# A four-layer graph network on one core: four of sixteen terms of the per-node sum moved to ScalarE and Pool, and the later layers' weights made inside an earlier product

## The chip, the cores and the metric

One core of a Trainium2 chip runs the whole program. The metric is the device time of one execution in microseconds (us). Five engines work side by side: TensorE (PE) multiplies matrices, VectorE (DVE) and ScalarE (ACT) work element by element, GpSimd (POOL) does some of that too and here issues most stores, SyncE (SP) issues loads. Each takes its instructions in a fixed order; a semaphore holds an instruction until its inputs are there and its output buffer is free. Matmul results lie in PSUM, everything else on chip in SBUF.

## The reference

Eight graphs of N = 2048 nodes with C = 64 features share one matrix A, the rows of `adj`. Each layer takes h = relu(layernorm(x)) and adds its result to x. Layer 0, which the change is about:

```python
w = jnp.einsum('nd,dkio->nkio', embedding, weight)      # D = 16, K = 3
b = jnp.einsum('nd,do->no', embedding, bias)
As = [I, A, 2.0 * (A @ A) - I]
x_g = jnp.einsum('knm,bmc->bnkc', jnp.stack(As), x)     # x is h here
out = jnp.einsum('bnki,nkio->bno', x_g, w) + b
```

So each node n has a weight of its own, a sum over d of `embedding[n, d]` times a common weight. Layer 1 runs three steps v = W2 relu(W1 [v, A v] + b1) + b2, layer 2 is A h with a linear map behind it, layer 3 is attention. All three come down here to products with A, small weight matrices and, in layer 3, a mean over the nodes. The weights that layers 1 and 2 use (products of W1, W2 and w_out, and their bias rows) don't depend on x; the program makes them once, in `make_weights`.

## The kernel before

**Tiling.** Two graphs side by side make a pair, since 2×64 features fill 128 partitions; there are NP = 4 pairs p. The nodes come in NB = 4 blocks nb of 512, a block being four tiles t of 128 nodes. A stays in SBUF as `BT`. `product` (L212) makes one block of A v for a pair: 32 matmuls, 16 chunks by two, since v is split into a high and a low part, `H` and `L` (`halves`, L199: ScalarE casts, VectorE subtracts). Its result in PSUM is scaled by the row `crow` (L209) on VectorE.

**Layer 0 of a pair.** First `term1` (L344): four products, which give t1 = A h for all nodes; each block is transposed back and split again for the second product. In pairs 2 and 3 this is a stage by itself; for pairs 0 and 1 the prologue makes t1. Then for each block nb: the product that gives t2 = A t1, then `node_weights` (L565). There, for each tile t and each half dg of the 16 values of d, PE makes

```python
y = psums[-1].tile([P, 2, 512], F32, tag="big", ...)    # two such buffers, L576
y[:, bb, :] = sum over k of terms[k][hs_, ts] x wt[hs_, k, dg * 512:(dg + 1) * 512]
```

that is, for 128 nodes and both graphs, what eight values of d would give (8×64 columns). Twelve matmul instructions make one y. Then VectorE adds the eight parts up, each scaled by the node's own embedding value, a column of one value per partition (L589):

```python
xj = (av, ov)[d % 2][:, t]                              # acc for even d, odd for odd d
nc.vector.scalar_tensor_tensor(xj, yd, ec, old, op0=ALU.mult, op1=ALU.add)
```

`acc` starts as x (loaded by `load_x`), `odd` starts as the bias block `bn` (loaded from `biasD`, two buffers). After the four tiles L597 adds `odd` to `acc`, and `keep` (L556) begins the norm for the next layer and stores x to `xs`. So a block has eight y tiles, and a layer 0 of 16 blocks 128 of them and 1,024 sums. The last block of all is different: between its tiles `prepare_next` already prepares layer 1.

**The norm.** `norm_stages` (L152) is a generator of three stages: mean and z (VectorE) and the square (ScalarE); the variance (VectorE) and `rstd` (a power on Pool, L169); z times rstd with the relu (L172), then the store of z to `hs` from Pool's queue. A stage is emitted whenever `go_on` (L182) is called: after a product and after each tile of `node_weights`.

**What sets the order.** The Tile framework places the instructions on each engine in the order in which the program emits them. `tc.issue_after(ins)` moves what is emitted inside it behind a named instruction, which then decides its place: `go_on` puts the norm's stages behind the last sum, and the store of the mask `MD` (L648) stands behind the store of `xs`. Waits follow from tiles: a reader waits for the writer, and the writer of a reused buffer for the readers of its last contents. Loads are on SP, in order (x, bias block, crow rows, h blocks); stores of `hs`, `xs`, `MD` and `wD` are issued by Pool, in order, between its own arithmetic.

**The weights.** `make_weights` (L471) is called once, for pair 3 ahead of block 1's product, and put behind the last sum of block 0 (`chain[-1]`):

```python
if p == NP - 1 and nb == 1:
    with tc.issue_after(chain[-1].ins):
        make_weights()
```

It loads eight columns and eight weight blocks (into `raw`, cleared by Pool first, L479), transposes them on PE (pt_wT, L484), copies them on VectorE (`tr`), multiplies four pairs on PE (wP, L490), copies the result (`pr`, L491), adds `b1s` (L493), loads the row `b_out` (L496) over what raw held and adds it (L497), and stores three parts to `wD` from Pool's queue (L504 to L506). Layers 1 and 2 load `wD` later. `raw`, `tr` and `pr` take the three buffers of the tag "z", which the norm's z uses as well; the PSUM tag "tr" has two buffers for all transposes.

Of the kernel before, what the change touches and what calls it, by code (L numbers as in the profile page):

```python
# [8 lines left out]
F32 = mybir.dt.float32  # L9
# [4 lines left out]
AF = mybir.ActivationFunctionType  # L14
ALU = mybir.AluOpType
# [27 lines left out]
def uniform_path(  # L43
# [30 lines left out]
    nc = tc.nc  # L74
    P = 128
    B, N, C = x.shape
    NP = B // 2
# [3 lines left out]
    DG = 512 // C  # L81
# [13 lines left out]
    hs = [dram.tile([P, NCH, 2 * C], F32, name=f"hs{p}") for p in range(NP)]  # L95
# [8 lines left out]
    def block(tag, name, bufs):  # L104

        return work.tile([P, 4, 2 * C], F32, tag=tag, name=name, bufs=bufs)
# [8 lines left out]
    def part(nb):  # L115
        return slice(4 * nb, 4 * nb + 4)
# [61 lines left out]
    def norm_relu(xt, name, done, out_=None):  # L178
        n = norm_stages(xt, name, done, out_)
        next(n)  # L180
        pending.append([n, 2])
# [12 lines left out]
        while pending:  # L194
            go_on()

    copies = []

    def halves(src, name, pool=None):  # L199

# [24 lines left out]
    def transposed(src, name):  # L225

        pt = psums[-1].tile([P, 4, P], F32, tag="tr", name=f"pt_{name}")
        for t in range(4):
            nc.tensor.transpose(pt[:, t, :], src(t), ident)  # L229
        return pt  # L230
# [11 lines left out]

    def term(k, name):
        pool = l0t if k == 1 else l0f[0]
        return pool.tile([P, 512], F32, tag=f"t{k}", name=name, bufs=(2, 4, 2)[k])

    def norm_0(p, nb, also=None, xt=None):

        def done(z):
            nc.gpsimd.dma_start(hs[p][:, part(nb), :], z)  # L250
            if also is not None:
                also(z)

        norm_relu(load_x(0, p, nb) if xt is None else xt, f"0_{p}_{nb}", done)
# [207 lines left out]
    def col(src, width, name, t=None):  # L462
        t = consts.tile([P, width], F32, name=name) if t is None else t
        for hf in range(2):
            nc.sync.dma_start(t[hf * C:(hf + 1) * C, :], src)
        return t
# [2 lines left out]
    b1s = consts.tile([P, 1], F32, name="b1s")  # L469

    def make_weights():  # L471
        col(b1[:, None], 1, "b1c", b1c)
        b2c = col(b2[:, None], 1, "b2c")
        bnl = col(b_nl[:, None], 1, "bnl")
        wn = col(w_nl, 2, "wnl")
        ws = consts.tile([P, 1], F32, name="wsum")

        raw, tr, pr = (block("z", f"wz{i}", 3) for i in range(3))
        nc.gpsimd.memset(raw, 0.0)  # L479
        for i, w in enumerate((w1[:, :C], w1[:, C:], w2, w_out)):  # L480
            for hf in range(2):
                hs_ = slice(hf * C, (hf + 1) * C)
                nc.sync.dma_start(raw[hs_, i, hs_], w)
        nc.vector.tensor_copy(tr, transposed(lambda t: raw[:, t, :], "wT"))  # L484
        nc.vector.tensor_copy(w1e, tr[:, 1])
        ps = psums[-1].tile([P, 4, P], F32, tag="tr", name="wP")
        b2b, bnb = b2c.to_broadcast([P, P]), bnl.to_broadcast([P, P])
        pairs = ((raw[:, 2], tr[:, 0]), (raw[:, 2], tr[:, 1]), (b2b, tr[:, 1]), (bnb, tr[:, 3]))
        for i, (lhsT, rhs) in enumerate(pairs):
            nc.tensor.matmul(ps[:, i, :], lhsT, rhs, start=True, stop=True)  # L490
        nc.vector.tensor_copy(pr, ps)  # L491
        p1 = bank("tr", "wb1s")
        nc.tensor.matmul(p1[:, :1], tr[:, 0], b2c, start=True, stop=True)  # L493
        nc.vector.tensor_tensor(b1s, p1[:, :1], b1c, op=ALU.add)

        fill_row(raw[:, 0, :], b_out)  # L496
        nc.vector.tensor_tensor(pr[:, 3, :], pr[:, 3, :], raw[:, 0, :], op=ALU.add)  # L497
        nc.vector.tensor_scalar(wn, wn, INV_SQRT2, None, op0=ALU.mult)
        nc.vector.tensor_tensor(ws, wn[:, 0:1], wn[:, 1:2], op=ALU.add)
        nc.vector.tensor_scalar(tr[:, 3, :], tr[:, 3, :], ws, None, op0=ALU.mult)  # L500
        fill_row(raw[:, 1, :], b2)
        for hf in range(2):
            nc.sync.dma_start(ivt[:, hf * C:(hf + 1) * C], iv)
        nc.gpsimd.dma_start(wD[:, 0:4], tr)  # L504
        nc.gpsimd.dma_start(wD[:, 4:8], pr)
        nc.gpsimd.dma_start(wD[:, 8:9], raw[:, 1:2, :])  # L506


    lastp = []
# [45 lines left out]

    def keep(p, nb, acc, name, more=None):  # L556

        norm_relu(acc, name, lambda z: nc.gpsimd.dma_start(hs[p][:, part(nb), :], z))
        if more is not None:
            nc.gpsimd.tensor_tensor(acc, acc, more, op=ALU.add)  # L560
        kept.append(nc.gpsimd.dma_start(xs[p][:, part(nb), :], acc))  # L561
# [2 lines left out]

    def node_weights(p, nb, terms, between=None):  # L565
        acc = load_x(0, p, nb)
        bn = l0q.tile([P, 4, C], F32, name="bn", bufs=2)
        nc.sync.dma_start(bn, biasD[:, part(nb), :])

        odd = l0q.tile([P, 4, 2 * C], F32, name="odd")  # L570
        av = acc.rearrange("p j (b c) -> p j b c", b=2)
        ov = odd.rearrange("p j (b c) -> p j b c", b=2)
        for t in range(4):
            ts = slice(t * P, (t + 1) * P)
            for dg in range(D // DG):
                y = psums[-1].tile([P, 2, 512], F32, tag="big", name=f"y_{p}_{nb}_{t}_{dg}")  # L576
                for k in range(K):
                    for bb in range(2):
                        hs_ = slice(bb * C, (bb + 1) * C)
                        nc.tensor.matmul(  # L580
                            y[:, bb, :], terms[k][hs_, ts], wt[hs_, k, dg * 512:(dg + 1) * 512],
                            start=(k == 0), stop=(k == K - 1),
                        )
                for d in range(DG):
                    e = dg * DG + d
                    yd, ec = y[:, :, d * C:(d + 1) * C], emb[:, 4 * nb + t, e:e + 1]
                    xj = (av, ov)[d % 2][:, t]
                    old = xj if e != 1 else bn[:, t, None, :].to_broadcast([P, 2, C])
                    last = nc.vector.scalar_tensor_tensor(  # L589
                        xj, yd, ec, old, op0=ALU.mult, op1=ALU.add  # L590
                    )
            ahead.append(last)
            chain.append(last)
            go_on()
            if between:
                between(t)
        nc.vector.tensor_tensor(acc, acc, odd, op=ALU.add)  # L597
        keep(p, nb, acc, f"1_{p}_{nb}")

    def feat_0(p, q):  # L600
# [4 lines left out]
    for p in range(NP):  # L605
        hl_next, t1T_next = [], []

        def prepare(q):

            nm = f"0_{p + 1}_{q}"  # L610
            if p == 0:
                src = l0q.tile([P, 512], F32, tag="hb", name=f"t1b_{nm}", bufs=2)
                nc.sync.dma_start(src, t1D[:, q * 512:(q + 1) * 512])
                hl_next.append(back(src, 1, q))
            elif p + 1 < NP:
                hl_next.append(halves(load_h(p + 1, q, nm, l0q), nm))

        def reload_t1(q):
            t = term(1, f"t1T_0_1_{q}")
            nc.sync.dma_start(t, t1D[:, q * 512:(q + 1) * 512])  # L620
            t1T_next.append(t)

        if p > 1:
            t1T, hl1 = term1(p, hl, lambda nb: norm_0(p + 1, nb) if p + 1 < NP else None)
        for nb in range(NB):
            nm = f"0_{p}_{nb}b"
            if p == NP - 1 and nb == 1:
                with tc.issue_after(chain[-1].ins):
                    make_weights()
            crow = load_crow(nb, nm)  # L630
            t2T = product(
                hl1, nb, nm, term(2, f"t2T_{nm}"), crow,
                fill={8: lambda: prepare(2)} if nb == 3 else {},
            )
            go_on()
            if nb == 3:
                prepare(3)
            t0T_next = feat_0(*divmod(4 * p + nb + 1, 4)) if 4 * p + nb + 1 < 4 * NP else None
            node_weights(
                p, nb, (t0T, t1T[nb], t2T),  # L640
                (lambda t: prepare_next(0, t)) if 4 * p + nb + 1 == 4 * NP else None,
            )
            t0T = t0T_next
            if nb in (1, 2):
                prepare(nb - 1)
            with tc.issue_after(kept[-1].ins):
                m = 4 * p + nb
                nc.gpsimd.dma_start(MD[m * P:(m + 1) * P, :], BTf[:, m, :])  # L648
            if p == 0:
                reload_t1(nb)  # L650
                norm_0(2, nb)
        if p == 0:
            hl1, t1T = hl_next, t1T_next
        else:
            hl = hl_next
# [767 lines left out]
```

## Time and profile before

| | |
|---|---|
| median of 3 runs | 1309.96 us (1307.51 to 1310.53) |
| profiled execution | 1313.01 us, of which the profile's span is 1310.9 us |
| TensorE's granted clock over the span | 0.983 of full speed |
| busy: PE, VectorE, ScalarE, Pool | 1229.1, 746.8, 188.6, 215.4 us |
| layer 0's blocks, from the first y product to the last | 116.5 to 674.9 us of the span |
| a product with A (32 matmuls) | 7.39 us |
| the eight y tiles of an undisturbed block | 20.97 us |

A row of the profile names a line of the kernel, an engine, an operation, the written and the read tile and their shapes, and how often it ran. Behind the bar stand its total busy time, the mean of one in nanoseconds, and the time for which the engine was idle just ahead of these instructions, with what ended most of that idle time (the releaser). Rows of the timeline begin with the start in us from the beginning of the span and the length; rows that follow each other without a gap may stand in one. The span is the time of the instructions seen; the execution's time has some 2 us more around it. TensorE's weight loads (PEld) overlap its matmuls and are listed apart.

### The profile page before, as it was taken

What the parts mean: (1) busy time and instruction counts of PE and PEld (TensorE: products, weight loads), DVE (VectorE), ACT (ScalarE), POOL (GpSimd) and SP (SyncE); (2) the same over time, 40 slices, a digit from 0 to 9 for tenths busy, and PEclk for the clock granted to TensorE, in tenths of its full rate; (3) what the DMA queues carried; (4) which work ended last, traced back from release to release, by engine and by line L of the source; (5) the groups of instructions that cost most, each with busy time, mean ns of one, the idle gap of its engine ahead of it and who ended that gap; (6) DMA issues with size and microseconds to landing.
All of it is one profiled execution on the core that took longest, in us unless ns stands there. A gap on an engine that the chain in (4) does not pass through costs nothing.

```text
span 1310.9 us, 15657 instructions
## 1 busy us (share of the span) xinstructions
PE 1229.1 (94%) x5702; PEld 863.9 (66%) x5702; DVE 746.8 (57%) x1941; ACT 188.6 (14%) x313; POOL 215.4 (16%) x222
## 2 busy tenths in 40 slices
PE   3699999899999999989999999999999999899994
PEld 2476555455585557645567887788787878678774
DVE  5325887677746785446754436345543644565554
ACT  4541001000010000000011121112112111111000
POOL 4210111111121111010101024004102400521111
PEclk9899999999999999999999999999999999999997
DMA  8793334322343232122246625533653552524431
GB/s 253 220 237 113 85 97 109 89 72 62 98 100 91 69 83 64 33 71 69 65 98 150 129 81 152 121 89 114 151 117 92 153 121 61 156 70 119 98 89 36
DMA packets 150842, 140.11 MB, mean 107 GB/s; under 512 B 100916, under 2 KB 102964, under 8 KB 150756
## 3 DMA queue, kind: packets, MB, share of 16 engines
q1 hardware_dynamic: 137780, 106.54, 31.9%
q0 software_dynamic: 9808, 31.70, 8.5%
q10 hardware_dynamic: 3168, 0.79, 0.3%
q8 instruction: 47, 0.77, 0.3%
q14 instruction: 39, 0.32, 0.1%
HBM read 94.87 MB, written 35.73 MB: 100 GB/s over the span
## 4 chain that ended last, share of the span: by engine, by line
PE 76%; DVE 7%; issue 6%; DMA 5%; POOL 3%; ACT 1%; SPq 1%; POOLq 0%; ACTq 0%; DVEq 0%
PE bv L217 33%; PE y L580 21%; PE bn L523 4%; PE ph L742 3%; PE bv_2b L217 2%; POOL rstd L169 2%; PE bv_3b L217 2%; PE bv_1b L217 1%; PE bv_0a L217 1%; DMA st<-in_adj_dram 1%; DMA hb<-hs 1%; PE bn_u L523 1%; DVE acc L589 1%; DVE odd L589 1%; PE pt L229 1%
## 5 line engine op out<-in xcount | busy, mean ns | idle before, releaser
L217 PE MATMUL bv<-BT,H 128*128 128x512 f32 x1024 | 426.3, 416 | 0.0
L217 PE MATMUL bv<-BT,L 128*128 128x512 f32 x1024 | 401.5, 392 | 0.0
L217 PEld LDWEIGHTS bv<-BT,H 128*128 128x128 f32 x1024 | 193.0, 188 | 48.1 <-issue 11.5
L217 PEld LDWEIGHTS bv<-BT,L 128*128 128x128 f32 x1024 | 193.1, 189 | 47.8 <-issue 11.5
L589 DVE SCALAR_TENSOR_TENSOR acc<-y,emb,acc 128x128 f32<-128x128 f32 x512 | 176.3, 344 | 70.3 <-PE y L580 66.1
L580 PE MATMUL y<-wt,t0T 64*128 64x512 f32 x512 | 146.0, 612 | 14.9 <-DVE odd L589 14.9
L589 DVE SCALAR_TENSOR_TENSOR odd<-y,emb,odd 128x128 f32<-128x128 f32 x448 | 153.4, 342 | 0.0
L169 POOL TENSOR_TENSOR rstd<-var,mhalf 128x8 f32<-128x8 f32 x64 | 106.0, 1658 | 219.5 <-DVE var L167 214.1
L209 DVE TENSOR_TENSOR g<-bv,crow 128x512 f32<-128x512 f32 x48 | 33.2, 692 | 182.3 <-PE bv L217 182.3
L163 ACT ACTIVATE sq<-z 128x512 f32<-128x512 f32 x64 | 40.4, 631 | 422.9 <-DVE z L159 410.9
L580 PEld LDWEIGHTS y<-wt,t0T 64*128 64x128 f32 x512 | 47.4, 188 | 78.7 <-issue 73.0
L560 POOL TENSOR_TENSOR acc<-acc,wl 128x512 f32<-128x512 f32 x16 | 21.0, 1315 | 294.9 <-DVE z L159 293.7
L172 DVE SCALAR_TENSOR_TENSOR z<-z,rstd 128x512 f32<-128x512 f32 x64 | 44.8, 706 | 42.7 <-POOL rstd L169 42.7
L580 PE MATMUL y<-wt,t1T 64*128 64x512 f32 x256 | 67.6, 594 | 0.0
L561 POOL DMA_DIRECT2D xs<-acc x32 | 17.9, 561 | 288.7 <-DVE acc L597 238.1
L523 PEld LDWEIGHTS bn<-wl,g 128*128 128x128 f32 x384 | 49.5, 191 | 6.2 <-ACT g L747 2.1
L166 DVE TENSOR_REDUCE var<-sq 128x8 f32<-128x512 f32 x64 | 43.5, 680 | 15.4 <-ACT sq L163 15.4
L523 PE MATMUL bn<-wl,g 128*128 128x128 f32 x384 | 51.1, 276 | 0.8 <-DVE var L167 0.8
L689 DVE SCALAR_TENSOR_TENSOR junk<-mt,cols,st 128x512 uint8<-128x512 bf16 x64 | 49.3, 770 | 0.5
L580 PEld LDWEIGHTS y<-wt,t1T 64*128 64x128 f32 x256 | 27.6, 187 | 27.5 <-issue 27.5
L747 ACT ACTIVATE g<-g,b1s 128x512 f32<-128x512 f32 x32 | 23.2, 724 | 139.5 <-DVE g L746 139.4
L159 DVE TENSOR_TENSOR z<-acc,mean 128x512 f32<-128x512 f32 x56 | 38.3, 691 | 6.3 <-DMA hs<-z 4.7
(206 smaller groups left out, 1674.9 us busy)
## 6 DMA issues: line engine op xcount, KB each, us to landing
st<-in_adj_dram SPq DMA_DIRECT2D x128, 256.0 KB, 4.0
crow<-crowD SPq DMA_DIRECT2D x64, 256.0 KB, 3.3
hs<-z POOLq DMA_DIRECT2D x48, 256.0 KB, 2.8
hb<-hs SPq DMA_DIRECT2D x40, 256.0 KB, 3.2
xs<-acc POOLq DMA_DIRECT2D x32, 256.0 KB, 2.4
MD<-BT POOLq DMA_DIRECT2D x16, 512.0 KB, 5.1
acc<-xs SPq DMA_DIRECT2D x32, 256.0 KB, 4.9
acc<-in_x_dram SPq DMA_DIRECT2D x48, 128.0 KB, 3.7
```

The source lines that it names most:

```text
L159: nc.vector.tensor_tensor(g, groups(xt), mean[:, :, None].to_broadcast([P, 8, C]), op=ALU.subtract)
L163: nc.scalar.activation(sq, z, AF.Square)
L166: nc.vector.tensor_reduce(var, groups(sq), axis=AX.X, op=ALU.add)
L169: powers.append(nc.gpsimd.tensor_tensor(rstd, var, mhalf, op=ALU.pow))
L172: nc.vector.scalar_tensor_tensor(groups(h), g, 0.0, rstd[:, :, None].to_broadcast([P, 8, C]), op0=ALU.max, op1=ALU.mult)
L209: ahead.append(nc.vector.tensor_tensor(out, ps, crow, op=ALU.mult))
L217: nc.tensor.matmul(ps, hl[m // 4][i][:, m % 4, :], BT[:, m, nb * 512:(nb + 1) * 512], start=(m == 0 and i == 0), stop=(m == NCH - 1 and i ...
L523: nc.tensor.matmul(ps[:, t, :], fT[:, t * P:(t + 1) * P], wmat, start=True, stop=True)
L580: nc.tensor.matmul(y[:, bb, :], terms[k][hs_, ts], wt[hs_, k, dg * 512:(dg + 1) * 512], start=(k == 0), stop=(k == K - 1),)
L589: last = nc.vector.scalar_tensor_tensor(xj, yd, ec, old, op0=ALU.mult, op1=ALU.add)
L689: nc.vector.scalar_tensor_tensor(junk, mt, cols[:, i, :], st, op0=ALU.mult, op1=ALU.not_equal, accum_out=bad[:, i, q:q + 1],)
L742: fill[12] = lambda: nc.tensor.matmul(ph, w1v2 if s else w1vT, gT[nb], start=True, stop=True)
```

## The change

Three things change in layer 0; layers 1 to 3 keep their code.

**The sum over d.** In each tile the order of d is now 6, 7, 0, 1, 2, 3, 4, 5. For d = 6 and 7, ScalarE multiplies the part of y by the embedding column (`activation` with `Copy` and `scale=ec`). The first of the four results of a node tile goes straight into a new block `rest`; the other three go to a small buffer `ye` (two of them), and Pool adds them to `rest`. VectorE does the other six as before. In all ScalarE gets 256 activations and Pool 192 adds, all of 128x128, and VectorE has 768 sums instead of 1,024, and one more add a block (acc and rest).

**The stores of hs** that a norm makes while `node_weights` runs are kept in a list and issued behind the last Pool add of tile 2. To make room, `bn` has one buffer instead of two, and the second term's tile t2 one instead of two.

**The weights.** `make_weights` is a generator. For pair 3 `term1` runs its first step (the loads and the clearing of `raw`) behind product 0, and the rest behind product 2.

```diff
     def term(k, name):
         pool = l0t if k == 1 else l0f[0]
-        return pool.tile([P, 512], F32, tag=f"t{k}", name=name, bufs=(2, 4, 2)[k])
+        return pool.tile([P, 512], F32, tag=f"t{k}", name=name, bufs=(2, 4, 1)[k])
...
         def done(z):
-            nc.gpsimd.dma_start(hs[p][:, part(nb), :], z)
+            def store():
+                nc.gpsimd.dma_start(hs[p][:, part(nb), :], z)
+
+            held[0].append(store) if held else store()
...
-        raw, tr, pr = (block("z", f"wz{i}", 3) for i in range(3))
+        raw = block("z", "wz0", 3)
         nc.gpsimd.memset(raw, 0.0)
         for i, w in enumerate((w1[:, :C], w1[:, C:], w2, w_out)):
             for hf in range(2):
                 hs_ = slice(hf * C, (hf + 1) * C)
                 nc.sync.dma_start(raw[hs_, i, hs_], w)
+        yield
+        tr, pr = (block("z", f"wz{i}", 3) for i in (1, 2))
...
-        norm_relu(acc, name, lambda z: nc.gpsimd.dma_start(hs[p][:, part(nb), :], z))
+        def store(z):
+            nc.gpsimd.dma_start(hs[p][:, part(nb), :], z)
+
+        norm_relu(acc, name, lambda z: held[0].append(lambda: store(z)) if held else store(z))
...
-        bn = l0q.tile([P, 4, C], F32, name="bn", bufs=2)
+        bn = l0q.tile([P, 4, C], F32, name="bn")
         nc.sync.dma_start(bn, biasD[:, part(nb), :])
+        held.append([])
         odd = l0q.tile([P, 4, 2 * C], F32, name="odd")
+        rest = l0q.tile([P, 4, 2 * C], F32, name="rest")
...
-                for d in range(DG):
+                for d in (6, 7, 0, 1, 2, 3, 4, 5):
                     e = dg * DG + d
                     yd, ec = y[:, :, d * C:(d + 1) * C], emb[:, 4 * nb + t, e:e + 1]
+                    if d > 5:
+                        first = e == 6
+                        ye = rv[:, t] if first else l0q.tile([P, 2, C], F32, name="ye", bufs=2)
+                        nc.scalar.activation(ye, yd, AF.Copy, scale=ec)
+                        if not first:
+                            add = nc.gpsimd.tensor_tensor(rv[:, t], rv[:, t], ye, op=ALU.add)
+                        continue
...
             go_on()
+            if t == 2:
+                with tc.issue_after(add.ins):
+                    for store in held.pop():
+                        store()
...
         nc.vector.tensor_tensor(acc, acc, odd, op=ALU.add)
+        nc.vector.tensor_tensor(acc, acc, rest, op=ALU.add)
...
         if p > 1:
-            t1T, hl1 = term1(p, hl, lambda nb: norm_0(p + 1, nb) if p + 1 < NP else None)
+            steps = make_weights()
+
+            def behind(nb):
+                if p + 1 < NP:
+                    norm_0(p + 1, nb)
+                elif nb in (0, 2):
+                    next(steps)
+
+            t1T, hl1 = term1(p, hl, behind)
...
-            if p == NP - 1 and nb == 1:
-                with tc.issue_after(chain[-1].ins):
-                    make_weights()
```

More of the change, by code (lines that the diff above doesn't have):

```diff
@@ L195, in all_done @@
             go_on()
-    copies = []
+    copies, held = [], []
     def halves(src, name, pool=None):
@@ L506, in make_weights @@
         nc.gpsimd.dma_start(wD[:, 8:9], raw[:, 1:2, :])
+        yield
     lastp = []
@@ L566, in node_weights @@
         acc = load_x(0, p, nb)
-        bn = l0q.tile([P, 4, C], F32, name="bn", bufs=2)
+        bn = l0q.tile([P, 4, C], F32, name="bn")
         nc.sync.dma_start(bn, biasD[:, part(nb), :])
+        held.append([])
         odd = l0q.tile([P, 4, 2 * C], F32, name="odd")
-        av = acc.rearrange("p j (b c) -> p j b c", b=2)
-        ov = odd.rearrange("p j (b c) -> p j b c", b=2)
+        rest = l0q.tile([P, 4, 2 * C], F32, name="rest")
+        av, ov, rv = (t.rearrange("p j (b c) -> p j b c", b=2) for t in (acc, odd, rest))
         for t in range(4):
```

## The prediction

> **What bounds the kernel now.** I read the page's shares first, then its costliest groups, the list of waits, the sums of three stretches, and the timeline of single tiles.
>
> ```profile
> PE 1229.1 (94%) x5702; PEld 863.9 (66%) x5702; DVE 746.8 (57%) x1941; ACT 188.6 (14%) x313; POOL 215.4 (16%) x222
> ...
> L589 DVE SCALAR_TENSOR_TENSOR acc<-y,emb,acc 128x128 f32<-128x128 f32 x512 | 176.3, 344 | 70.3 <-PE y L580 66.1
> L580 PE MATMUL y<-wt,t0T 64*128 64x512 f32 x512 | 146.0, 612 | 14.9 <-DVE odd L589 14.9
> ```
>
> TensorE is busy 94% of the span. Over all blocks it waits for the sums of L589 only 14.9 us, while VectorE's sums wait 66.1 us for TensorE.
>
> ```profile
> core 0: us, PE busy (x) PEld busy (x) DVE busy (x) ACT busy (x) POOL busy (x), PEclk, DMA share, GB/s
> ...
> 569.86:606.62 36.76, 30.43 (x116) 13.27 (x115) 18.88 (x66) 0.88 (x2) 3.89 (x5) 0.91 0.19 58
> 614.54:635.53 20.99, 20.99 (x98) 9.64 (x97) 16.76 (x60) 0.59 (x1) 2.26 (x2) 1.00 0.19 51
> ```
>
> Both stretches are the y products of one block, the same 96 matmuls. The clean one (pair 3, block 2) is solid PE; the one with the later weights in it (block 1) is 15.8 us longer, and its clock is lower. Its cause stands in the waits and in the timeline:
>
> ```profile
> PE y L580 <- DVE odd L589: 14.9, 8, 5.7
> ...
> DVE wz L491 <- DMA wD<-wz: 8.1, 1, 8.1
> ```
>
> ```profile
> 587.69 0.69 DVE L491 COPY wz<-wP 128x512 f32<-128x512 f32 x1 [8.05 <-DMA wD<-wz]
> ...
> 590.80 2.08 PE L580 MATMUL y<-wt,t0T 64*128 64x512 f32 x4 [5.70 <-DVE odd L589]
> ```
>
> VectorE stood 8.05 us before L491 with the next y sums queued behind it; so both y buffers stayed full and PE stood 5.70 us. Then its matmuls ran at half pace (2.08 us for four, against 1.03 below). The clean tile, with its sums:
>
> ```profile
> 598.75 1.03 PE L580 MATMUL y<-wt,t0T 64*128 64x512 f32 x4
> 598.96 0.35 DVE L589 SCALAR_TENSOR_TENSOR acc<-y,emb,acc 128x128 f32<-128x128 f32 x1 [0.48 <-PE y L580]
> ...
> 600.78 0.34 DVE L589 SCALAR_TENSOR_TENSOR odd<-y,emb,odd 128x128 f32<-128x128 f32 x1
> ...
> 601.32 0.65 PE L580 MATMUL y<-wt,t0T 64*128 64x512 f32 x2
> ```
>
> PE takes 601.32−598.75 = 2.57 us a tile. Eight sums start 0.26 us apart and end at 601.12. After a real wait PE started 0.14 to 0.15 us behind the last sum (150.81 to 150.95, 246.79 to 246.94, 590.65 to 590.80), so here the buffer is free at about 601.27, and PE wanted it at 601.32: **0.05 us of slack.**
>
> **Part 1: a quarter of the sums leaves VectorE.** 256 sums at 344 ns are 88 us of VectorE's busy time. In a clean block none of it is on the path, so it counts nothing by itself. It does relieve the blocks in which VectorE was late. Three y blocks of pair 0 take 21.59 us where clean ones take 20.97, and four of pairs 1 and 2 (starting at 237.6, 272.3, 391.9, 421.8) 26.75, 22.90, 21.97 and 22.84. There I take two sums of 0.26 off each of the seven: **−3.6 us** (0 to −5). What else the four wait for is an H cast behind a load, which stays.
>
> **Part 2: a new wait.** Both engines read the same y. In the changed order the first VectorE sum of each tile waits for ScalarE, and the first matmul into a buffer waits for both. So a tile's chain becomes: PE's end, two activations, six sums, PE. Behind the waiting sum stand the other five and the norm's stages; for the last of the sums PE waits. Six sums take 5×0.26+0.34 = 1.64 us. The trace has no activation of 128x128 from PSUM with a scale by column. Nearest rows:
>
> ```profile
> L747 ACT ACTIVATE g<-g,b1s 128x512 f32<-128x512 f32 x32 | 23.2, 724 | 139.5 <-DVE g L746 139.4
> ...
> L234 ACT COPY t0T<-pt 128x512 f32<-128x512 f32 x16 | 9.4, 586 | 59.0 <-PE pt L229 59.0
> ...
> L813 ACT ACTIVATE ex<-y 128x128 f32<-128x128 f32 x4 | 1.2, 311 | 21.0 <-DVE y L812 21.0
> ```
>
> L163, 512 wide without a column operand, takes 631; L747 with one 724, so a column costs 93. A read from PSUM is cheaper by 35 (L234's 586 against L204's 621 from SBUF). Hence 311+93−35 = **0.37 us, the value I take, nearest to the row of the same shape**; lower bound 311−35 = 0.28, upper bound a 512-wide row, 0.587+0.093 = 0.68. Consecutive activations of L294 start 0.52 us apart at 0.624 each, an overlap of 0.10. A pair is then 0.64 us (0.45 to 1.26). With 0.03 us for each handover (as PE's end to the first sum now) the release is at 598.95+0.64+0.03+1.64+0.15 = 601.41, later than PE's natural 601.32 by δ = 0.09. A late tile gives the next one room, so δ counts at every second tile from the third on: 3 a block, 15 blocks (the last block's tiles are longer by 2.8 us, bound by PE). With some 0.04 us to refill PE each time (pair 0's late blocks lose 0.62 where PE's idle row shows 0.42 behind matmuls that otherwise overlap by 0.17): 45×0.13 = **+6 us**. Bounds: a pair of up to 0.55 costs 0; at 1.26, δ is 0.71 and the sum 45×0.75 = +34.
>
> The Trainium skill, "PSUM — Partial Sum Buffer", section "PSUM bank collisions raise a hardware error", says that ScalarE and VectorE must not touch one bank in the same partitions at once, and that a dependency keeps them apart. That speaks against the change: the activations precede the sums instead of running beside them, and without the rule the chain would be no longer than the six sums, making the +6 a 0. No row of this trace shows two engines at one y. The page "ScalarE: Activation LUTs", section "What ACT_TABLE_LOAD costs", gives 186 ns + 0.833 ns an element and 93 ns a column operand; that would make an estimate of 0.39 us an activation, and 45×0.17 = 7.6 instead of 6.
>
> **Part 3: Pool's 192 adds.** No add of 128x128 is in the trace. L560, 128x512, takes 1315 ns: upper bound; the 128x128 select of the identity takes 290: lower; I take 0.4 by shape. At three in 5.15 us even the upper bound fits, and two ye buffers let ScalarE run ahead: 0. The stores of hs that once stood here wait for the ninth add, so that no add stands behind a store that waits for VectorE. They land some 10 us later; they are read a pair later at the earliest. Pool's adds do slow some VectorE operations: L172's 0.69 us stretched to 1.13 and 1.33 beside L560 or L721, while those with a PSUM operand (L723, L746) stayed at 683 to 688. So not the sums, but z by about an add: **+1 us** (0 to 2). The extra add of acc and rest (0.69 us a block) replaces two sums and lies beside the next product, where VectorE is idle 1.9 to 3 us: 0.
>
> **Part 4: buffers.** With one bn, block k+1's load starts when block k's last use ends, over 7 us ahead of its use (landing 2.6): 0. t2 is written only after the product that follows all readers: 0. Should bn be late, a sum waits some 2 us a block, +30.
>
> **Part 5: weights inside term1 of pair 3.** Block 1 of pair 3 falls from 36.76 to the clean 20.99 us: −15.8, of which I count **−15.4** (0.4 in case PE doesn't find the block quite clean). In term1 the weights cost: four transposes, 0.35 (as PE's from 517.12 to 517.47 there), and five 128-wide matmuls, 0.28 each in L523's row, 0.85 with overlap; the wait of wP for VectorE's copy, 0.69 and two handovers, 0.8; and L497 stands behind a row load that took 5.7 us to land before, with the fourth chunk's L behind it in turn: 0 to 2.6, I take 0.5. Together **+2.5** (+1.4 to +5). SP issues eight loads (0.6 to 0.8 us each) ahead of crow for product 2: it lands at about 518.5 and is needed at 524.8. Pool's memset stands after the stores of pair 2, its three wD stores before the first adds: 0. Layers 1 to 3 need wD 100 us later.
>
> **Sum.** 1313.0 (the profiled execution; span 1310.9) −3.6 +6 +1 −15.4 +2.5 = 1303.5, or −9.5. The median of the runs shown is 1309.96, 3 us below the profiled one; on it **1300.5**.
>
> **Rivals.** (a) *The ScalarE link decides (slower).* If one activation takes 0.48 us or more, a pair 0.86, then δ = 0.31 and 45×0.35 = +15.8 against the −12.9 of part 5 and the +1 of Pool, with the relief of part 1 gone, makes +3.9; that is the point from which it is slower by 0.3%. At 0.53 us: +19.8+1−12.9 = +7.9, 1318; at the upper bound +22, 1332. For it: only 0.05 us of slack, and every tile passes ScalarE. Against: the row of the same shape is 0.31. (b) *The link is free.* A pair within 0.55: −12.9−3.6+1 = −15.5, 1294; with the cheapest term1 1293. (c) *The weights' wait only moves.* The eight loads and the row loads make VectorE wait in term1 as before, about 8 us, with products queued behind it: −15.4+1.4+8 = −6, in all −6−3.6+6+1 = −2.6, 1307: no change. Against: PE has products to do that need nothing of it. (d) *The change isn't doing what it says*: Pool, behind a store, holds ye, so that ScalarE and then y wait; 16 blocks by 0.5 us, 1308; against, no add stands behind a store that waits for VectorE.
>
> **Chances.** Forecast (1297 to 1305) 0.50; (b) 0.17; (a) 0.18; (c) 0.10; (d) 0.05. A measurement can tell about 0.3%, 4 us, from no change: faster 0.70 (forecast, b, part of c), same 0.12, slower 0.18. The range leaves out the tail of (a) beyond 0.53 us and of (b): 1292 to 1318; 1292 to 1306 on the faster side.
>
> **What would show it.** Block 1 of pair 3 near 21 us; no wait at L491 above 1 us; term1 of pair 3 longer by 2 to 3 us; y blocks of 20.97 + 0.4; activations at 0.37 (at 0.48 the forecast falls); "PE y" waits of about 0.1 us, 45 of them. The prediction is wrong if adds take over 1.3 us, if a sum of L589 takes over 0.36, if VectorE waits in term1 for the row load, or if the y blocks grow by a microsecond.

## The result, and the profile after

The changed kernel takes 1310.0 us (median of 4 runs, 1309.5 to 1310.81) against 1309.98 us before: ratio 1.0004, with a 95% interval of 0.9987 to 1.0022. No change, where 1300.5 was forecast. The profiled execution took 1310.81 us, its span is 1309.0 us. The profiled execution of the kernel before lay 3.0 us above its median, this one 0.8, so the two profiles below differ by 2.2 us though the medians agree.

The page of the kernel after, engines and the groups that the change touches (L608 is the old L589, L592 the old L580):

```profile
PE 1231.1 (94%) x5702; PEld 861.7 (66%) x5702; DVE 693.1 (53%) x1701; ACT 267.3 (20%) x569; POOL 303.6 (23%) x414
...
L608 DVE SCALAR_TENSOR_TENSOR acc<-y,emb,acc 128x128 f32<-128x128 f32 x384 | 132.6, 345 | 143.6 <-ACT ye L602 136.5
L592 PE MATMUL y<-wt,t0T 64*128 64x512 f32 x512 | 147.7, 624 | 12.2 <-DVE odd L608 12.1
...
L604 POOL TENSOR_TENSOR rest<-rest,ye 128x128 f32<-128x128 f32 x192 | 87.2, 454 | 264.8 <-ACT ye L602 259.5
```

VectorE is busy 54 us less (256 sums at their spacing of 0.26, less 16 adds of 0.69), and TensorE's share of the span is the same. What VectorE's sums wait for has changed: no longer the matmuls, but ScalarE's `ye`, 136.5 us. The sums of three stretches of the kernel after (term1 of pair 3, its block 1, its block 2; columns as in the prediction):

```profile
509.55:550.21 40.66, 40.66 (x197) 33.44 (x195) 14.16 (x29) 3.60 (x7) 6.43 (x10) 1.00 0.30 83
579.64:604.43 24.79, 21.70 (x97) 9.68 (x96) 13.14 (x46) 5.13 (x16) 6.81 (x12) 1.00 0.23 54
612.36:633.89 21.53, 21.53 (x97) 9.57 (x96) 13.22 (x46) 4.96 (x15) 6.80 (x12) 1.00 0.25 58
```

Block 1 fell from 36.76 to 24.79 us, not to 21; a clean block grew from 20.99 to 21.53. Layer 0, stage by stage in the two profiles (us):

| | forecast | measured |
|---|---|---|
| weights: block 1 of pair 3 without its stall, term1 and the product behind it | −12.9 | −13.7 (−15.8 +1.7 +0.4) |
| eight clean blocks (block 1 of pair 3 counted as one): the link through ScalarE | +3.1 | +4.5 |
| the seven late blocks of pairs 0 to 2: link less relief | −0.9 | +4.1 |
| block 1 of pair 3, beyond the link | 0 | +3.3 |
| Pool beside VectorE; the gap ahead of pair 0's block 3 | +1 | −1.1 |
| sum | −9.7 (−9.5 with the rounding there) | −2.9 |

Ahead of layer 0 the profiled run of after lost 1.2 us; the start of the first y product lies anywhere from 114.9 to 118.8 us in the runs of this case, so this is no part of the change. The gain forecast for the weights was there. The link through ScalarE cost a little more than forecast, block 1 of pair 3 kept a stall of 3.3 us, and the late blocks lost instead of gaining. Why the gap ahead of pair 0's block 3 (9.77 us for 10.85) got shorter isn't shown.

### The profile page after: what moved, and what is told of

It is laid out like the page before. It is cut to its first block, busy times and chain, and to the rows that moved or that the text cites. A ratio compares the mean times of both kernels' runs of the same rounds, so it can differ in the third digit from the quotient of the medians.

```text
span 1309.0 us, 16102 instructions
## 1 busy us (share of the span) xinstructions
PE 1231.1 (94%) x5702; PEld 861.7 (66%) x5702; DVE 693.1 (53%) x1701; ACT 267.3 (20%) x569; POOL 303.6 (23%) x414
## 4 chain that ended last, share of the span: by engine, by line
PE 79%; DVE 7%; DMA 6%; POOL 3%; issue 2%; ACT 1%; SPq 1%; ACTq 0%; POOLq 0%; DVEq 0%
PE bv L217 31%; PE y L592 24%; PE bn L530 4%; PE ph L772 3%; POOL rstd L169 2%; PE bv_2b L217 2%; PE bv_3b L217 2%; DMA st<-in_adj_dram 2%; PE bv_0b L217 2%; DMA hb<-hs 1%; PE bv_0a L217 1%; PE bv_3a L217 1%; PE bv_2a L217 1%; PE bv_1a L217 1%; PE bn_u L530 1%
## 5 line engine op out<-in xcount | busy, mean ns | idle before, releaser
L217 PEld LDWEIGHTS bv<-BT,H 128*128 128x128 f32 x1024 | 193.0, 188 | 48.2 <-issue 11.6
L608 DVE SCALAR_TENSOR_TENSOR acc<-y,emb,acc 128x128 f32<-128x128 f32 x384 | 132.6, 345 | 143.6 <-ACT ye L602 136.5
L592 PE MATMUL y<-wt,t0T 64*128 64x512 f32 x512 | 147.7, 624 | 12.2 <-DVE odd L608 12.1
L604 POOL TENSOR_TENSOR rest<-rest,ye 128x128 f32<-128x128 f32 x192 | 87.2, 454 | 264.8 <-ACT ye L602 259.5
L608 DVE SCALAR_TENSOR_TENSOR odd<-y,emb,odd 128x128 f32<-128x128 f32 x320 | 109.7, 343 | 0.0
L592 PEld LDWEIGHTS y<-wt,t0T 64*128 64x128 f32 x512 | 46.3, 187 | 83.4 <-issue 66.7
L602 ACT ACTIVATE ye<-y,emb 128x128 f32<-128x128 f32 x192 | 63.0, 362 | 124.8 <-PE y L592 123.4
L592 PE MATMUL y<-wt,t1T 64*128 64x512 f32 x256 | 68.4, 600 | 0.0
L172 DVE SCALAR_TENSOR_TENSOR z<-z,rstd 128x512 f32<-128x512 f32 x64 | 44.7, 704 | 43.8 <-POOL rstd L169 43.7
L777 ACT ACTIVATE g<-g,b1s 128x512 f32<-128x512 f32 x32 | 23.2, 724 | 139.6 <-DVE g L776 139.5
L602 ACT ACTIVATE rest<-y,emb 128x128 f32<-128x128 f32 x64 | 23.5, 367 | 134.7 <-PE y L592 120.7
```

The lines of the kernel that those rows point to most:

```text
L172: nc.vector.scalar_tensor_tensor(groups(h), g, 0.0, rstd[:, :, None].to_broadcast([P, 8, C]), op0=ALU.max, op1=ALU.mult)
L217: nc.tensor.matmul(ps, hl[m // 4][i][:, m % 4, :], BT[:, m, nb * 512:(nb + 1) * 512], start=(m == 0 and i == 0), stop=(m == NCH - 1 and i ...
L592: nc.tensor.matmul(y[:, bb, :], terms[k][hs_, ts], wt[hs_, k, dg * 512:(dg + 1) * 512], start=(k == 0), stop=(k == K - 1),)
L602: nc.scalar.activation(ye, yd, AF.Copy, scale=ec)
L604: add = nc.gpsimd.tensor_tensor(rv[:, t], rv[:, t], ye, op=ALU.add)
L608: last = nc.vector.scalar_tensor_tensor(xj, yd, ec, old, op0=ALU.mult, op1=ALU.add)
```

## The experiments

**Theory L**: the weights' move brings what was forecast; the offload gives it back, because ScalarE now stands in the chain of every y tile, and what waits at the head of its queue holds the tiles up. **Rival W**: the weights' move is worth little. **Rivals within L** (does the amount of ScalarE's work count, its place, or the wait as such?) stand at the experiments.

### The two halves apart

`weights_only` is the kernel before with the generator `make_weights` of the diff; `sum_only` the kernel after with

```diff
-                elif nb in (0, 2):
-                    next(steps)
...
+            if p == NP - 1 and nb == 1:
+                with tc.issue_after(chain[-1].ins):
+                    list(steps)
```

> The kernel before with only the weights moved into the last pair's term1. Theory L (the weights' move brings what was forecast for it; the offload of the sums gives it back, because ScalarE stands in the chain of every y tile and its queue can hold a tile up): block 1 of pair 3 falls from 36.76 to 21 us, term1 grows by 1.7 us, all other blocks stay as before; 1310 - 15.8 + 1.7 = 1296 us. Rival W (the weights' move itself is worth little, because its loads and PE work only change place): 1304 us or more.

> The changed kernel with the weights made at their old place, before block 1 of pair 3. Theory L: clean blocks 21.54 instead of 20.97, the blocks with an H cast at their head 1 to 2.5 us longer than before, block 1 of pair 3 near 37 us; in all 8 to 11 us slower than before: 1318 to 1321 us. Rival W: within 4 us of before.

Measured: `weights_only` 1297.7 us against 1309.29, ratio 0.9911 (0.9896 to 0.9926); `sum_only` 1315.65, ratio 1.0050 (1.0033 to 1.0067), less than I had expected. Block 1 of pair 3 in `weights_only`:

```profile
566.86:587.85 20.99, 20.99 (x97) 9.65 (x97) 16.75 (x60) 0.88 (x2) 2.26 (x2) 1.00 0.22 57
```

Block 1 is clean to the hundredth, and term1 takes 40.66 us, solid PE, as in the kernel after. Rival W falls. The halves don't add up, though: 0.9911×1.0050 = 0.9960, and both together give 1.0004, some 5.8 us more, give or take 4. Something costs only where both are there. The profiles say where: block 1 of pair 3 takes 36.76 us before, 20.99 with the weights moved, 35.47 with the sums moved, so 19.7 if the two added up; it takes 24.79, 5.1 us more.

### The copy at the head of ScalarE's queue

ScalarE's timeline in block 1 of pair 3, kernel after:

```profile
579.75 0.58 ACT L234 COPY t0T<-pt 128x512 f32<-128x512 f32 x1 [1.62 <-PE pt L229]
585.39 0.30 ACT L546 COPY hb<-ivt 1x128 f32<-1x128 f32 x1 [5.06 <-DMA hb<-hs]
585.59 0.35 ACT L602 ACTIVATE rest<-y,emb 128x128 f32<-128x128 f32 x1
```

and TensorE's:

```profile
584.03 1.02 PE L592 MATMUL y<-wt,t2T_1b 64*128 64x512 f32 x4
588.02 1.13 PE L592 MATMUL y<-wt,t0T 64*128 64x512 f32 x4 [2.96 <-DVE odd L608]
```

The copy of one row, `ivt`, is layer 1's work for the block `hb`. The program emits it with the last block of layer 0, in `prepare_next`; on ScalarE it stands two blocks earlier, 4 us behind the issue of its load. So the order of emission isn't the order of the queue, as was told above. In the kernel before it waits at the same place (585.9, 4.67 us), and nothing wants ScalarE then; VectorE's own stall for the weights covers it besides. In the kernel after the activations of the first y tile stand behind it. `ivt_late` ties the copy to the last block:

```diff
+                if n == 0:
+                    nc.vector.scalar_tensor_tensor(
+                        ivt, accs0[-1][0:1, 0, :], 0.0, ivt, op0=ALU.mult, op1=ALU.add
+                    )
                 nc.scalar.copy(h[0:1, 0, :], ivt)
```

> The changed kernel, with the one-row copy of ivt on ScalarE made to depend on the last block's first sums, so that it no longer stands ahead of the activations of pair 3's block 1 (one small VectorE operation more, the same values). Theory L (in order queue of ScalarE): that block falls from 24.79 to 21.54 us, all else as in the changed kernel: 1306.7 us. Rival (the 5.4 us for which VectorE waits there is the weights' work in another form, such as Pool's wD stores behind the row load): it stays at 24 to 25 us.

Measured: 1305.28 us, ratio 0.9973 (0.9962 to 0.9985). The block, from its sums:

```profile
575.17:596.71 21.54, 21.54 (x97) 9.57 (x97) 13.22 (x46) 4.97 (x15) 6.82 (x12) 1.00 0.24 60
```

From 24.79 to 21.54 as expected: this is 3.25 of the 5.1 us that the halves alone don't show (the tie itself costs 1.08 us in the last block). The rest is what the weights' stall hides in `sum_only`: the link, and 1.29 us by which the block, at 35.47, is shorter there than before. That run came out below my 1318 in part because the copy costs nothing behind that stall.

### What a clean block loses

The late tile in the kernel after (pair 3, block 2; weight loads left out, and sums between the first and the last):

```profile
617.76 1.13 PE L592 MATMUL y<-wt,t0T 64*128 64x512 f32 x4
...
620.41 1.05 PE L592 MATMUL y<-wt,t0T 64*128 64x512 f32 x4
620.64 0.37 ACT L602 ACTIVATE rest<-y,emb 128x128 f32<-128x128 f32 x1 [2.13 <-PE y L592]
620.91 0.36 ACT L602 ACTIVATE ye<-y,emb 128x128 f32<-128x128 f32 x1
...
621.30 0.35 DVE L608 SCALAR_TENSOR_TENSOR acc<-y,emb,acc 128x128 f32<-128x128 f32 x1 [0.52 <-ACT ye L602]
...
622.60 0.34 DVE L608 SCALAR_TENSOR_TENSOR odd<-y,emb,odd 128x128 f32<-128x128 f32 x1
...
623.09 0.70 PE L592 MATMUL y<-wt,t0T 64*128 64x512 f32 x2
```

y is ready at about 620.61, the pair ends at 621.27, the sums start 0.03 us later and end at 622.94, TensorE starts 0.15 us behind: 2.48 us from y to release, as forecast (2.46). TensorE could have started at 620.41+2.57 = 622.98, so it is 0.11 us late. It loses more than that: the tile behind a late one starts 2.65 us later (617.76 to 620.41), not 2.57, and more than every second tile is held: in this block the first matmul stands 0.15 or 0.16 us behind the sum that frees its buffer in five of the last six. The tiles follow each other by 2.65 to 2.72 us, where it was 2.57 to 2.68. The Trainium skill, "PSUM — Partial Sum Buffer", section "PSUM bank collisions raise a hardware error", has the dependency between ScalarE and VectorE at one bank; the trace agrees, the first sum starting 0.03 to 0.04 us after the pair's end in each tile of this block.

Three experiments ask what sets this loss. `fixed_scale`: `scale=ec` becomes `scale=0.5`.

> The changed kernel with the activation's scale a constant 0.5 instead of the embedding column; so four of sixteen terms are scaled wrongly and everything else stays. Theory L (the latency of two activations in the chain sets the 0.57 us that clean blocks lose): an activation falls from 0.362 to about 0.27 us, a pair's part of the chain by 0.09 to 0.18 us, which is all or nearly all of the 0.11 us by which the next matmul is late; clean blocks fall to 20.97 to 21.1 us, the total by 5 to 7 us: 1303 to 1305. Rival S (the wait itself costs: one more semaphore on TensorE and VectorE a tile, whatever the latency): blocks stay at 21.5.

Measured: 1298.81 us, ratio 0.9922 (0.9903 to 0.9941). Its activations, and the same block:

```profile
L602 ACT ACTIVATE ye<-y 128x128 f32<-128x128 f32 x192 | 46.1, 274 | 134.9 <-PE y L592 133.8 <-POOL rest L604 1.0
```

```profile
599.82:620.82 21.00, 21.00 (x98) 9.64 (x97) 13.22 (x46) 3.71 (x15) 6.83 (x12) 1.00 0.25 61
```

274 ns instead of 362 (the Trainium skill, "ScalarE: Activation LUTs", section "What ACT_TABLE_LOAD costs", has 93 for a column operand; 88 here), and the loss is gone whole. So it is the chain's latency, not the wait as such: rival S falls, and the pair up to which the link is free lies between 0.45 us (here) and 0.62 (the kernel after), where the forecast had 0.55. The total fell below the 1303 to 1305 expected; beside the clean blocks, pair 1's block 1 is 22.57 us for 25.48 (the last section has why that block was so long). And even with the link free the kernel is no faster than `weights_only`, which leaves the offload out (1297.7). Blocks 2 and 3 of pair 0 also fall by 0.54 us below the kernel before (21.46 and 21.05): the relief that part 1 forecast is there when the link isn't.

`one_term` leaves one term to ScalarE, `sums_first` the old order of d:

```diff
-                for d in (6, 7, 0, 1, 2, 3, 4, 5):
+                for d in (7, 0, 1, 2, 3, 4, 5, 6):
...
-                    if d > 5:
-                        first = e == 6
+                    if d > 6:
+                        first = e == 7
```

```diff
-                for d in (6, 7, 0, 1, 2, 3, 4, 5):
+                for d in range(DG):
```

> The changed kernel with only one of eight terms of a y tile on ScalarE (d = 7), seven sums on VectorE, the same values. Theory L (a chain through both engines, in which each activation takes the place of a sum): one activation 0.37 and 7 sums 6x0.26+0.34 = 1.89 instead of a pair 0.62 and 6 sums 1.64, both 2.26 us; so clean blocks stay at 21.5 us, within 0.1. Rival A (the loss goes with the amount of ScalarE's work): half the loss, 21.25 us. Under L the stall of 3.2 us in pair 3's block 1 stays as well.

> The changed kernel with the order of d unchanged (0 to 7), so that VectorE's six sums come first and ScalarE's two activations last, the same values. Theory L (the two engines' parts add up, whichever is first): clean blocks 21.4 to 21.7 us, TensorE's idle rows now released by ScalarE. Rival O (the place of ScalarE ahead of the sums is what costs): 20.97 us. Beside it: with the sums first, VectorE is not held by what stands on ScalarE's queue, but TensorE is; so the 24.8 us of pair 3's block 1 should stay under L.

Measured, one run each: 1314.05 and 1309.78 us. The same block in `one_term`, then in `sums_first`:

```profile
612.79:634.32 21.53, 21.53 (x97) 9.56 (x97) 15.02 (x53) 3.16 (x8) 3.64 (x5) 1.00 0.26 62
```

```profile
612.39:633.74 21.35, 21.35 (x98) 8.70 (x97) 13.22 (x46) 4.97 (x15) 6.42 (x12) 1.00 0.24 56
```

Half the terms on ScalarE, the same 21.53 us: an activation follows the next by 0.26 or 0.27 us, a sum by 0.26, so moving terms doesn't shorten the chain by anything, while the second engine adds a start of 0.1 and a handover. Rival A falls. With the sums first 21.35: nearly the same, a little outside what I had expected, and rival O's 20.97 doesn't come. Block 1 of pair 3 keeps its stall in `one_term` (24.47 us); in `sums_first` it is 22.69, not the 24.8 expected: the sums are done by then, and TensorE waits 1.25 us for the two activations alone, instead of 2.96 for activations and sums. The first blocks of pairs 1 and 2 are longer in `sums_first`, 22.3 to 28.2 us.

### The add and the loads behind it

In the kernel before, the x store ahead of pair 1's block 1 and SP's loads behind it (block from 272.29):

```profile
267.66 0.54 POOL L561 DMA_DIRECT2D xs<-acc  x1 [16.75 <-DVE acc L597]
```

```profile
270.09 1.66 SPq L126 DMA_DIRECT2D acc<-in_x_dram  x2
272.39 0.48 SPq L135 DMA_DIRECT2D hb<-hs  x1
```

In the kernel after (block from 273.88):

```profile
270.21 0.56 POOL L571 DMA_DIRECT2D xs<-acc  x1 [2.61 <-DVE acc L622]
```

```profile
272.65 1.65 SPq L126 DMA_DIRECT2D acc<-in_x_dram  x2
274.40 1.05 SPq L135 DMA_DIRECT2D hb<-hs  x1
```

The H casts of the two blocks, before and after:

```profile
275.89 0.62 ACT L204 CAST H<-hb 128x512 fp32r<-128x512 f32 x1 [2.92 <-DMA hb<-hs]
```

```profile
278.49 0.62 ACT L204 CAST H<-hb 128x512 fp32r<-128x512 f32 x1 [3.92 <-DMA hb<-hs]
```

The store waits for the added addition L622 and came 4.63 us ahead of the block before, 3.67 now. The x load waits for the stored buffer, the h load stands behind it on SP: issued 0.10 us into the block before, 0.52 now. The H cast waits for it, VectorE's L for the cast, and the tile's activations and sums stand behind both: cast at 3.60 us before, 4.61 after, the block 22.90 and 25.48 us. The sums start behind VectorE's L (279.14 in the kernel after, the first sum at 279.75), as before; the activations were done by 279.64, so here ScalarE's queue isn't what they waited for. In pair 0's block 1 the x load itself is late: VectorE's first sum waits for it until 4.69 us into the block, 3.31 before.

TensorE's waits for the sums in the seven late blocks come to 9.2 us before and 9.1 after (14.9 and 12.1 in all, less the 5.70 and 2.96 of pair 3's block 1). Four blocks wait 0.4 to 0.5 us less, as the relief has it; pair 0's block 1 (+0.87) and block 1 of pairs 1 and 2 (+0.49, +0.33) wait longer. `no_rest_add` leaves L622 out, so that four of sixteen terms are missing.

> The changed kernel without the one addition of rest to acc a block; so four of sixteen terms are missing in the output and everything else stays. Theory X (that add and the later last tile put off the store to xs, behind it the x load into the freed buffer and, in SP's order, the h load for which the casts and with them the y tiles of pairs 1 and 2 wait): the store comes 0.7 us earlier, at about 4.4 us ahead of the next block instead of 3.65; the h load of block 1 of pairs 1 and 2 is issued at 0.1 to 0.2 us instead of 0.5, and these blocks are 0.5 to 2 us shorter; clean blocks stay at 21.54. Rival: the h load stays where it is.

Measured: 1305.52 us, ratio 0.9957 (0.9942 to 0.9972), against 1.0004 with the add. The x store comes 4.44 us ahead, the h load at 0.10 and 0.11 us in pairs 1 and 2; their block 1 takes 23.51 and 23.02 us, where the kernel after had 25.48 and 23.59; pair 0's block 1 falls from 23.03 to 21.95, block 1 of pair 3 from 24.79 to 23.83; clean blocks stay at 21.54. The rival falls. TensorE's waits in these four and in pair 1's block 0 are 3.7 us shorter in all. Against that pair 0's block 3 is 1.7 us longer (23.23, at a clock of 0.93) and the gap ahead of it 1.2. The lengths of these blocks swing by up to 3 us with the same code: pair 1's block 0 took 26.75 us in the kernel before and 23.65 in `weights_only`, about half of it in the wait (3.90 and 2.35 us, set by the loads' landing), half in the matmuls behind it, slowed in the one and not in the other. So the 6 us between the ratios is the better measure, and it is no better than 3 us either way; the profiles' layer 0 gives 4.3.

### The casts taken from the head of the blocks

The same waits stand in the kernel before: four blocks of pairs 1 and 2 take 22.0 to 26.8 us. `weights_hb3` gives the h blocks three buffers (and t2 one) beside the moved weights; `weights_pin` ties their casts to the block just ended; `weights_best` does both, the tie for the first two only; `sum_pin` is `ivt_late` with that tie (`accs0` lists each block's acc).

```diff
-    t = pool.tile([P, 4, 2 * C], F32, tag="hb", name=f"hb_{name}", bufs=2)
+    t = pool.tile([P, 4, 2 * C], F32, tag="hb", name=f"hb_{name}", bufs=3 if pool is l0q else 2)
...
-                hl_next.append(halves(load_h(p + 1, q, nm, l0q), nm))
+                h = load_h(p + 1, q, nm, l0q)
+                if q < 2:
+                    late = accs0[-1][0:1, 0, 0:1]
+                    nc.vector.scalar_tensor_tensor(
+                        h[0:1, 0, 0:1], late, 0.0, h[0:1, 0, 0:1], op0=ALU.mult, op1=ALU.add
+                    )
+                hl_next.append(halves(h, nm))
```

> The weights moved, the sums as before, and three instead of two buffers for the h blocks (one t2 buffer makes the room). Theory Q (the four long blocks of pairs 1 and 2 wait for a load whose buffer comes free only at the block's start, with casts and sums queued behind it): they fall from 23.6 to 26.8, 22.3 to 22.9, 22.0 and 22.8 us to about 21, the total by 5 to 9 us against the weights alone: 1289 to 1293. Rival: the casts are placed earlier as well and wait as long there: 1297, no change.

> The weights moved, the sums as before, and the casts of the next pair's h blocks made to depend on the block just ended (a one-element VectorE operation that adds zero times its sum, the same values), so that they can't stand at the head of an earlier block. Theory Q: the same four blocks fall to about 21 to 21.6 us, the total by 5 to 9 us against the weights alone: 1289 to 1293. Rival: later casts hold the two h buffers longer, so that the next block's transposes wait on TensorE instead: 1297 or more.

> The weights moved, the sums as before, three buffers for the h blocks, and the casts of the next pair's first two h blocks tied to the block just ended. Theory Q (each of the two had removed the waits of four blocks and made one elsewhere: with three buffers block 3 of pair 0 at 25.1 us, with the tie alone block 3 of pairs 1 and 2 at 25.6): together no block of pairs 0 to 2 is over 22.1 us; 1286 to 1292 us. Rival: the loads only find a new place to be late; a block over 23 us is left, 1293 or more.

> The changed kernel with both queue waits taken away: the copy of ivt tied to the last block (as in ivt_late) and the casts of the next pair's first two h blocks tied to the block just ended (as in weights_best, but with two h buffers, since three don't fit beside the new tiles). Theory L+Q (what the offload costs is 0.55 us of chain a block, plus casts and loads ahead of the activations): the first blocks of pairs 1 and 2, now 21.9 to 26.7 us, all come to 21.5 to 21.7; block 1 of pair 3 is 21.54; block 3 of pairs 1 and 2 grows by 2 to 5 us, since its casts come later; the total is 1300 to 1304 us. Rival: a first block stays over 22.5 us, and the loss there has another cause.

Measured: 1294.17 us, ratio 0.9863 (0.9847 to 0.9879); 1296.94, 0.9880 (0.9863 to 0.9896); 1290.67, 0.9844 (0.9826 to 0.9862); 1306.62, 0.9963 (0.9950 to 0.9976). With three buffers three of the four blocks fall to 21 to 22 us, but a cast moved ahead makes pair 0's block 3 25.12, and the total misses the 1293 expected. With the tie all four fall to 21.0 to 21.6, but block 3 of pairs 1 and 2 takes 25.6, waiting for the later casts' buffers: the theory was right on the four blocks, the rival on the total. Together every block of pairs 0 to 2 is at 21.0 to 22.0 but for block 3 of pairs 1 and 2, 23.2 (so "no block over 22.1" failed, and the rival's block over 23 was there, while the total came within the 1286 to 1292 of the theory). What is left of y's waits for VectorE in `weights_best`:

```profile
PE y L584 <- DVE odd L593: 1.6, 4, 0.4
```

In `sum_pin` the four blocks come to 21.53 or 21.54, one of them as

```profile
265.77:287.31 21.54, 21.54 (x98) 9.58 (x97) 13.22 (x46) 4.96 (x15) 6.81 (x12) 1.00 0.25 59
```

so with the casts out of the way nothing but the link is left there; its block 3 of pairs 1 and 2 takes 27.6 and 27.2, more than expected, and the total, 1306.6, is over the 1300 to 1304 expected. `weights_best` beats both kernels: 20.6 us below the one before.

## Why the prediction was wrong

Of the 9.5 us forecast, the profiles show 2.9 in layer 0 and the medians none. The steps that failed are part 2 (what stands ahead of the activations, +3.3 us, and the number of late tiles, about +1), part 1 (a relief of 3.6 us of which 0.1 was left) and part 3 (the extra add, put at 0).

- **Part 5 (weights) was right.** −13.7 in the profile for −12.9, 11.6 us in the medians of `weights_only`; rival (c) did not come.
- **Part 2 was right in its mechanism and in the clean tile** (activation 0.362 us for 0.37, release 2.48 for 2.46, PE late by 0.11 for 0.09). The count was short: 3 late tiles by 0.13 make 0.39 us a block, where five of the last six tiles are held by the sums, not every second one, and a clean block lost 0.55. Rival (b), a free link, falls with it.
- **Part 2 failed in naming what stands ahead.** It listed what is queued behind the waiting sum on VectorE; it did not look at what is queued ahead of the activations on ScalarE. The copy of `ivt` cost 3.25 us (`ivt_late`).
- **Part 1 failed.** TensorE's waits in the seven blocks fell by 0.1 us, not 3.6. Four blocks had 0.4 to 0.5 us of relief, and the link took most of it: pair 0's blocks 2 and 3 gained 0.05 instead of 0.5 (0.54 in `fixed_scale`). "What else the four wait for … stays" was wrong: it grew in block 1 of pairs 1 and 2, and in pair 0's block 1 as well.
- **Part 3's extra add was costed at 0 and was not.** The cover named, VectorE's idle time in the next product, was there; but the store of x waits for the add, and behind the store stand two loads and a cast. Leaving it out is worth some 6 us, give or take 3.
- **Pool's adds** took 0.454 us for 0.4. The +1 was not seen: no z of layer 0 (L172) ran beside one of them, and none took over 0.69 us. ScalarE waited for Pool to free a `ye` 1.4 us in all, so rival (d) did not come either.
- **Rival (a)** was nearer in what it made of the whole, a gain eaten by the offload, but not in the way: an activation of 0.36 us was well below its 0.48. The link took some 7 us for the 6 forecast; the rest went to the copy, the later loads and a slower clock behind one wait.

The late blocks' +4.1 us can be divided by the profiles: waits −0.1, slowed matmuls in pair 1's block 1 +1.7 (last section; pair 1's block 0 was slowed in both profiles), and +2.5 left for the link in seven blocks, near the 2.7 that the forecast's count gives. What stays open: how far the waits swing from one execution to the next with the loads' landing, which was not varied by itself, and what decides whether the matmuls slow down behind a wait.

## What to carry to other kernels

ScalarE was busy 14% of the span before, and it wasn't free: what counts is what waits at the head of its queue at the moment when the new work comes, and an instruction that waits there harmlessly becomes a stall for all that is put behind it. Where two engines read a buffer in turn and a term takes as long on either (0.26 us here), moving terms from one to the other doesn't shorten the time until it is released; it adds a start and a handover, and with 0.05 us of slack that is on the path. An add that hides beside a product can still hold up the store, the buffer and the loads behind it: follow its result to the last reader before costing it at nothing.

## What the hardware showed unexpectedly

TensorE's pace after a wait doesn't follow from the wait's length alone. In the kernel after, behind 2.24 us of waiting, the matmuls slowed down after a microsecond and were back 4 us later:

```profile
281.53 1.13 PE L592 MATMUL y<-wt,t0T 64*128 64x512 f32 x4 [2.24 <-DVE odd L608]
282.47 1.51 PE L592 MATMUL y<-wt,t1T 64*128 64x512 f32 x4
283.70 1.98 PE L592 MATMUL y<-wt,t2T_1b 64*128 64x512 f32 x4
285.41 1.52 PE L592 MATMUL y<-wt,t0T 64*128 64x512 f32 x4
286.74 1.05 PE L592 MATMUL y<-wt,t1T 64*128 64x512 f32 x4
```

The granted clock over that block is 0.93. Behind the 2.96 us at 588.02, shown above, they did not slow down, and the block's clock is 1.00. In the kernel before the same block's wait was shorter, with no slowing behind it:

```profile
279.45 1.13 PE L580 MATMUL y<-wt,t0T 64*128 64x512 f32 x4 [1.75 <-DVE odd L589]
```

Three groups of four are followed 1.23, 1.71 and 1.33 us later by the next, where it is 0.86 undisturbed: 1.7 us lost, of the 2.6 by which this block grew. Other runs have the same: slowed behind 2.03 us (`ivt_late`) and 2.07 (`sum_only`) in pair 2's block 1, not behind 2.70 (`no_rest_add`), 3.28 (`ivt_late`) and 3.31 (`sum_only`) in pair 1's block 0. What decides it isn't shown.
